# A two-layer graph kernel: bias products in half rows, and another order of the first group's set-up

## The chip, the core and the metric

The kernel runs on one core of a Trainium2 chip. Its time is the device time of one execution in microseconds (us); lower is better. The median of three runs of the kernel before is 1076.81 us (1076.48 to 1078.67).

A core has five engines with queues of their own: PE (TensorE, matrix products, with PEld for its weight loads), DVE (VectorE), ACT (ScalarE), POOL (GpSimd) and SP (SyncE, used here to issue DMAs only). Matrix products read SBUF and write PSUM.

## The reference

There are 128 graphs of 128 nodes with 64 features. Cut to what matters, for each graph:

```python
h   = relu(layernorm(x))
mask = adj > 0
z   = relu(h_j @ W1a + (h_j - h_k) @ W1b + b1)      # for every pair j, k; 192 wide
hm  = sum over k of mask[j, k] * z[j, k]
x   = x + hm @ W2 + deg[j] * b2
h   = relu(layernorm(x))
x   = x + (adj @ h) @ W.T
```

About one in eight of the adjacency entries is nonzero, so a row j has some 16 neighbours k.

## The kernel before

The 128 graphs are worked in 32 groups of G = 4. Inside a group, z is not computed for all pairs. Each quarter of 32 nodes k gives a row j up to D = 6 slots, and one-hot tiles S select the neighbour of each slot; neighbours beyond the sixth become "extra edges" (tiles R, RT, S2, X).

The group's main work is a list of T = 24 jobs. A job's `fill` lets TensorE form 768 columns of slot sums from the stacked tiles k3 and S3 (`g<-S,k` and `g<-id,k` in the profile); its `drain` reduces them on DVE (kind 0, `hm<-g`) or on ACT and then POOL (kind 1, `T<-g`, `T<-T`). Jobs of kind 1 use products 64 columns wide, two side by side. Three buffers of PSUM (`gtile`) are shared by the jobs, by the projections `pp` and by `pr`.

Between the jobs, pieces of other stages are run by three tables that name a job index and functions: AHEAD (set-up of the next group), OWN (extra edges of this group) and BEHIND (the finish of the group before). The set-up functions, in AHEAD's order, are:

- `pre_adj`: transposes the adjacency (`pt`), copies it (`adjT`), makes the mask (`maskT`), takes the statistics of x (`norm_a`)
- `pre_norm`: the normalised h
- `pre_rank`, `pre_slots`: the rank of each neighbour in its quarter (`pq`, `qs`), overflow `ov`, six slot tiles `S`, and 12 DMAs on SP's queue that copy S to `S3`
- `pre_hT`, `pre_count`: h transposed (`hT`); degree and number of overflows per row (`pd`, copied to `dn`, `nb`)
- `pre_proj` for r = 0 and 1: h times the joined weights `wp` (448 columns, float32), plus a bias product; split in three bfloat16 parts `ca` by ACT, DVE and POOL
- `pre_stack`: 12 DMAs on SP's queue that copy `ca` to `k3`, by quarter q and then by part
- `pre_edge_a`, `pre_place`, `pre_edge_b`, `pre_edge_d`, `pre_ra`, `pre_pads`, `pre_edge_c`: one-hot tiles of extra edges and corrections

TensorE's instructions are kept in the program's order (`mm`, `tp`, lines 181 and 184); the instructions of the other engines are put in order by the scheduler of the tile framework. Before the first job, all of AHEAD is run for group 0, one function after the other, after the weights have been loaded by 14 DMAs on ACT's queue and joined on DVE and TensorE.

The bias product adds `bias` to the projection exactly: its three bfloat16 parts stand in rows 0, 32 and 64 of `biasp`, the other rows are zero, and a tile of ones `oneb` sums over all 128 rows. It is run once for each half p of the partitions, after the two products with `wp`, which use 64 rows each:

```python
for p in range(2):
    s = slice(p * F, (p + 1) * F)
    mm(pp[:, p, 0 : 2 * H + O], d["hT"][s, r], wp[s, :], start=True, stop=False, ...)
for p in range(2):
    mm(pp[:, p, H : 2 * H + O], oneb, biasp, start=False, stop=True, ...)
```

Of the kernel before, what the change touches and what calls it, by code (L numbers as in the profile page):

```python
# [8 lines left out]
F32 = mybir.dt.float32  # L9
# [141 lines left out]
def kernel(  # L151
# [26 lines left out]
    nc = tc.nc  # L178
# [4 lines left out]
    def tp(*args, **kw):  # L183
        return tc.keep_in_program_order(nc.tensor.transpose(*args, **kw))  # L184
# [24 lines left out]
    with ExitStack() as main:  # L209
# [11 lines left out]
        def mtile(name):  # L221
            return ps_m.tile([P, 512], F32, tag="m", name=name)


        ident = const.tile([P, P], F32, tag="ident", name="ident")
        make_identity(nc, ident)
        identb = const.tile([P, P], BF16, tag="identb", name="identb")
# [8 lines left out]
        eps = const.tile([P, 1], F32, tag="eps", name="eps")  # L236
        nc.gpsimd.memset(eps, EPS)
# [27 lines left out]
        nc.vector.tensor_scalar(ioe, iov, BIG, None, ALU.add)  # L265


        wa2 = const.tile([P, H], F32, tag="wa2", name="wa2")
        wb2 = const.tile([P, H], F32, tag="wb2", name="wb2")
        w2a = const.tile([C0, O], F32, tag="w2a", name="w2a")  # L270
        w2h = const.tile([C0, O], F32, tag="w2h", name="w2h")
        w2bd = const.tile([P, 2, O], F32, tag="w2bd", name="w2bd")
        wl1 = const.tile([P, P], F32, tag="wl1", name="wl1")
# [5 lines left out]
        nc.vector.memset(w2bd, 0.0)  # L279
        nc.vector.memset(wl1, 0.0)  # L280
        for p in range(2):
            s = slice(p * F, (p + 1) * F)
            nc.scalar.dma_start(wa2[s, :], W1[0:F, :])
            nc.scalar.dma_start(wb2[s, :], W1[F : 2 * F, :])
            nc.scalar.dma_start(w2bd[s, p, :], W2[C0:H, :])
            nc.scalar.dma_start(wl1[s, s], W)
            nc.scalar.dma_start(b1d[s, :], b1[C0:H].unsqueeze(1))
        nc.scalar.dma_start(w2a, W2[0:C0, :])
        nc.scalar.dma_start(b2s, b2.unsqueeze(0).to_broadcast([P, O]))
        nc.scalar.dma_start(bias[:, 0:H], b1.unsqueeze(0).to_broadcast([P, H]))  # L290
        nc.scalar.dma_start(b1c, b1[0:C0].unsqueeze(1))
        nc.vector.tensor_scalar(w2h, w2a, 0.5, None, ALU.mult)

        wp = const.tile([P, 2 * H + O], F32, tag="wp", name="wp")
        wab = wp[:, H : 2 * H]
        nc.vector.tensor_scalar(wp[:, 0:H], wb2, -1.0, None, ALU.mult)
        nc.vector.tensor_tensor(wab, wa2, wb2, ALU.add)
        pw = mtile("pw")
        tp(pw[:, 0:P], wab[:, 0:C0], ident)
        wT = one.tile([P, P], F32, tag="wT", name="wT")  # L300
        nc.vector.tensor_copy(wT, pw[:, 0:P])
        pc = mtile("pc")
        mm(pc[:, 0:O], wT, w2h, start=True, stop=True)
        nc.vector.tensor_copy(wp[:, 2 * H : 2 * H + O], pc[:, 0:O])
        b1x = one.tile([P, P], F32, tag="b1x", name="b1x")
        nc.vector.tensor_copy(b1x, b1c.to_broadcast([P, P]))
        pb = mtile("pb")
        mm(pb[:, 0:O], b1x, w2h, start=True, stop=True)
        nc.vector.tensor_tensor(bias[:, H : H + O], pb[:, 0:O], b2s, ALU.add)
        pl = mtile("pl")  # L310
        tp(pl[:, 0:P], wl1, ident)
        nc.vector.tensor_copy(wl1t, pl[:, 0:P])

        biasp = const.tile([P, H + O], BF16, tag="biasp", name="biasp")
        nc.vector.memset(biasp, 0.0)
        left = bias
        for i in range(3):
            pt = one.tile([P, H + O], BF16, tag=f"bp{i}", name=f"bp{i}")
            nc.vector.tensor_copy(pt, left)
            nc.vector.tensor_copy(biasp[i * 32 : i * 32 + 1, :], pt[i * 32 : i * 32 + 1, :])  # L320
            if i < 2:
                nxt = one.tile([P, H + O], F32, tag=f"br{i}", name=f"br{i}")
                nc.vector.tensor_tensor(nxt, left, pt, ALU.subtract)
                left = nxt

        groups: dict[int, dict] = {}

# [15 lines left out]
        def norm_b(src, mv, to, u):  # L343

            sd = tmp.tile([P, G], F32, tag="sd", name=f"sd{u}")
            nc.scalar.activation(sd, mv[:, :, 1], AF.Sqrt, bias=eps)
# [17 lines left out]
        def pre_adj(g):  # L364
            d = groups[g]
            pt = mtile(f"pt{g}")
            for b in range(G):
                tp(pt[:, b * N : (b + 1) * N], d["adj"][:, b, :], ident)
            d["adjT"] = grp.tile([P, G, N], F32, tag="adjT", name=f"adjT{g}", bufs=3)
            nc.scalar.activation(  # L370
                d["adjT"].rearrange("k b j -> k (b j)"), pt, AF.Copy
            )
            d["maskT"] = grp.tile([P, G, N], BF16, tag="maskT", name=f"maskT{g}")
            nc.vector.tensor_scalar(d["maskT"], d["adjT"], 0.0, None, ALU.is_gt)
            d["mv"] = norm_a(d["x"], f"a{g}")

        def pre_norm(g):
            d = groups[g]
# [47 lines left out]
        def pre_count(g):  # L426
            d = groups[g]

            pd = mtile(f"pd{g}")
            for b in range(G):  # L430
                mm(
                    pd[:, b : b + 1], d["maskT"][:, b, :], oneb[:, 0:1], start=True, stop=True
                )
                mm(
                    pd[:, G + b : G + b + 1], d["ov"][:, b, :], oneb[:, 0:1], start=True, stop=True
                )
            d["dn"] = grp.tile([P, 2, G], F32, tag="dn", name=f"dn{g}")
            nc.vector.tensor_copy(d["dn"].rearrange("j t b -> j (t b)"), pd[:, 0 : 2 * G])  # L438
            d["nb"] = tmp.tile([P, G], BF16, tag="nb", name=f"nb{g}")
            nc.vector.tensor_copy(d["nb"], d["dn"][:, 1])  # L440

        def pre_pads(g):
            d = groups[g]
# [16 lines left out]
        def pre_proj(g, r):  # L460
# [7 lines left out]
            for p in range(2):  # L468
# [3 lines left out]
                    start=True, stop=False, skip_group_check=True,  # L472
                )
            for p in range(2):
                mm(
                    pp[:, p, H : 2 * H + O], oneb, biasp,
                    start=False, stop=True, skip_group_check=True,
                )
            x = pp[:, :, 0 : 2 * H].rearrange("n p (t u) -> n p t u", t=2)
# [16 lines left out]
        def pre_stack(g):  # L496

            d = groups[g]
            d["k3"] = grp.tile([K3, Q, 2, G, H], BF16, tag="k3", name=f"k3{g}")
            for q in range(Q):  # L500
                for part in range(3):
                    nc.sync.dma_start(
                        d["k3"][part * QN : (part + 1) * QN, q],
                        d["ca"][q * QN : (q + 1) * QN, part],
                    )
# [28 lines left out]
        def pre_edge_a(g):  # L534
            d = groups[g]
            pv = mtile(f"pv{g}")
            mm(pv[:, 0:G], upb, d["nb"], start=True, stop=True)
            mm(pv[:, G : 2 * G], oneb, d["nb"], start=True, stop=True)
            nc.vector.tensor_tensor(ovf, ovf, pv[:, G : 2 * G], ALU.max)

            d["half"] = tmp.tile([P, G], F32, tag="half", name=f"half{g}")
            nc.vector.tensor_scalar(d["half"], d["dn"][:, 1], -0.5, 0.5, ALU.mult, ALU.add)
# [276 lines left out]
        def pieces(table, t, g):  # L819
            if 0 <= g < NG:  # L820
                for f in table.get(t, ()):
                    f(g)
# [54 lines left out]
```

## Time and profile before

| | before |
|---|---|
| median of three runs, us | 1076.81 |
| the profiled execution's own time, us | 1076.04 |
| its span (first to last instruction), us | 1074.3 |
| mean granted TensorE clock | 0.987 |
| PE busy, us (share) | 1035.5 (96%) |
| PEld busy | 731.8 (68%) |
| DVE busy | 843.3 (79%) |
| ACT busy | 684.1 (64%) |
| POOL busy | 717.6 (67%) |
| PE instructions | 10438 products, 10438 weight loads |

Some groups of the page: `g<-S,k` 2048 products, 383.4 us; `g<-id,k` 4096, 381.3; `pp<-wp,hT` 256, 67.8; `pp<-biasp,oneb` 128, 25.3 (mean 280 ns). A float32 product appears as two passes. The durations of products overlap, as each is counted from its issue to its modelled end; the starts tell the pace. Some DMA rows, from issue to landing: S 192 KB, 4.0 us; k 96 KB, 2.2; adj 256 KB, 2.8; x 128 KB, 2.7; bias 96 KB, 4.1; b1c 0.5 KB, 3.9; b2s 32 KB, 3.6; wa 48 KB, 2.8; wb 48 KB, 3.1.

In a view's rows, L181 and L184 are the two helpers that record every product and transpose, so a product is told by its tiles. "SPq" is SP's queue issuing a DMA, "[0.29 <-PE pb L181]" an idle time before an instruction and what ended it.

### The profile page before, as it was taken

The numbers are of one execution on the slowest core, as the hardware profiler recorded it, in microseconds if no ns is written. First come the engines' busy times: TensorE is split into PE (matmuls) and PEld (weight loads), VectorE is DVE, ScalarE is ACT, GpSimd is POOL, SyncE is SP. The second block draws the span as 40 slices with busy tenths as digits, with TensorE's granted clock in tenths as the row PEclk, the third lists the DMA queues.
The fourth block names the chain that finished last, engine by engine and source line by source line (L and its number), as shares of the span: only waits on it lengthen the run. The fifth ranks groups of instructions, "written<-read, shape, count | busy, mean of one in ns | idle before, by whom it ended". The sixth has DMA issues, their size and how long they took to land.

```text
span 1074.3 us, 27146 instructions
## 1 busy us (share of the span) xinstructions
PE 1035.5 (96%) x10438; PEld 731.8 (68%) x10438; DVE 843.3 (79%) x1955; ACT 684.1 (64%) x1473; POOL 717.6 (67%) x810
## 2 busy tenths in 40 slices
PE   3699999999999999999999999999999999999995
PEld 1477776777677677677677677677777777667773
DVE  5468888878888878887877888877888887888763
ACT  4366666676666677666667666667666667666652
POOL 1377666777666687666686766677766677666674
PEclk9799999999999999999999999999999999999998
DMA  4456655456655456655456655445665545664420
GB/s 104 114 138 144 140 126 115 112 130 149 138 125 124 111 120 153 141 124 134 102 118 147 143 131 130 114 112 138 144 142 125 115 114 127 146 141 109 108 66 13
DMA packets 89062, 132.29 MB, mean 123 GB/s; under 512 B 47584, under 2 KB 64352, under 8 KB 88928
## 3 DMA queue, kind: packets, MB, share of 16 engines
q1 hardware_dynamic: 87552, 130.08, 53.0%
q8 instruction: 84, 1.38, 0.5%
q10 hardware_dynamic: 1376, 0.43, 0.2%
q14 instruction: 50, 0.41, 0.1%
HBM read 13.01 MB, written 4.19 MB: 16 GB/s over the span
## 4 chain that ended last, share of the span: by engine, by line
PE 93%; DVE 2%; SPq 2%; DMA 1%; ACT 1%; POOL 1%; issue 0%; ACTq 0%; POOLq 0%; DVEq 0%
PE g L181 49%; PE pe L181 7%; PE pp L181 7%; PE py L181 7%; PE px L181 6%; PE pr L181 3%; PE po L181 2%; PE pga L181 2%; PE pn L181 2%; PE pt L184 1%; PE pj L181 1%; PE pgq L181 1%; PE pq L181 1%; SPq L407 1%; DVE S L401 1%; PE pty L184 1%
## 5 line engine op out<-in xcount | busy, mean ns | idle before, releaser
L761 DVE TENSOR_REDUCE hm<-g 128x64 f32<-128x768 f32 x512 | 469.8, 949 | 115.7 <-PE g L181 113.5
L784 POOL TENSOR_TENSOR T<-T 128x768 f32<-128x768 f32 (+2 forms) x384 | 442.1, 1151 | 144.4 <-ACT T L771 126.8
L181 PEld LDWEIGHTS <-k 96*128 96x128 bf16 (+1 forms) x6144 | 408.5, 103 | 150.7 <-issue 37.2
L181 PE MATMUL g<-S,k 96*128 96x384 bf16 (+1 forms) x2048 | 383.4, 331 | 6.3 <-DMA k<-ca 5.1
L181 PE MATMUL g<-id,k 96*128 96x192 bf16 (+1 forms) x4096 | 381.3, 246 | 0.0
L771 ACT ACTIVATE T<-g 128x768 f32<-128x768 f32 x256 | 202.9, 805 | 25.4 <-PE g L181 23.4
L494 POOL TENSOR_TENSOR ca<-rest,ca 128x768 bf16<-128x768 f32 x64 | 105.0, 1642 | 170.5 <-ACT ca L493 161.1
L401 DVE TENSOR_SCALAR S<-qs 128x512 bf16<-128x512 bf16 x192 | 116.5, 675 | 3.0 <-issue 0.5
L483 ACT ACTIVATE ca<-pp 128x768 bf16<-128x768 f32 x64 | 51.3, 801 | 102.9 <-PE pp L181 99.0
L181 PE MATMUL pe<-RT,X 128*128 128x128 f32 (+1 forms) x512 | 79.4, 299 | 0.0
L493 ACT ACTIVATE ca<-rest 128x768 bf16<-128x768 f32 x64 | 53.7, 840 | 25.1 <-DVE rest L485 25.1
L181 PE MATMUL pp<-wp,hT 64*128 64x448 f32 x256 | 67.8, 607 | 1.9 <-DVE dn L438 1.9
L485 DVE TENSOR_TENSOR rest<-pp,ca 128x768 f32<-128x768 f32 x64 | 59.9, 936 | 4.5 <-ACT ca L483 4.5
L181 PEld LDWEIGHTS pe<-RT,X 128*128 128x128 f32 (+1 forms) x512 | 52.1, 164 | 9.8 <-issue 5.2
L668 ACT ACTIVATE ys<-py 128x256 f32<-128x256 f32 x32 | 12.3, 383 | 65.8 <-PE py L181 65.8
L456 POOL TENSOR_TENSOR ra<-ra,np 64x256 f32<-64x256 f32 x64 | 51.6, 806 | 2.4
L181 PE MATMUL px<-ca,S 128*128 128x192 bf16 x384 | 53.0, 247 | 0.0
L181 PE MATMUL px<-ca,R 128*128 128x192 bf16 x384 | 52.6, 246 | 0.0
L181 PEld LDWEIGHTS <-oneb 128*128 128x128 bf16 x192 | 13.5, 97 | 56.1 <-issue 56.1
L352 ACT ACTIVATE h<-x,mra,rsa 128x64 f32<-128x64 f32 x128 | 48.8, 435 | 3.7 <-DVE mra L350 2.2
L612 ACT ACTIVATE X<-px 128x256 f32<-128x256 f32 x64 | 24.5, 383 | 38.7 <-PE px L181 34.9
L181 PEld LDWEIGHTS <-R 128*128 128x128 bf16 x512 | 43.6, 98 | 7.9 <-issue 0.6
(130 smaller groups left out, 1425.0 us busy)
## 6 DMA issues: line engine op xcount, KB each, us to landing
S<-S SPq DMA_DIRECT2D x384, 192.0 KB, 4.0
k<-ca SPq DMA_DIRECT2D x384, 96.0 KB, 2.2
adj<-in_adj_dram SPq DMA_DIRECT2D x32, 256.0 KB, 2.8
x<-in_x_dram SPq DMA_DIRECT2D x32, 128.0 KB, 2.7
out_dram<-ot SPq DMA_DIRECT2D x32, 128.0 KB, 2.0
wa<-in_L_gnn_W_dram ACTq DMA_DIRECT2D x2, 48.0 KB, 2.8
wb<-in_L_gnn_W_dram ACTq DMA_DIRECT2D x2, 48.0 KB, 3.1
bias<-in_L_gnn_b_dram ACTq DMA_DIRECT2D x1, 96.0 KB, 4.1
```

Of the source, the lines that this page charges most:

```text
L181: return tc.keep_in_program_order(nc.tensor.matmul(*args, **kw))
L352: nc.scalar.activation(to(b), src[:, b, :], AF.Relu, bias=mr[:, b : b + 1], scale=rs[:, b : b + 1])
L401: nc.vector.tensor_scalar(d["S"][:, i, :], d["qs"].rearrange("k b j -> k (b j)"), float(i) + BIG, None, ALU.is_equal,)
L456: nc.gpsimd.tensor_tensor(d["ra1"][s], d["ra1"][s], d["np0"][s, 2 * p : 2 * p + 2], ALU.mult)
L483: nc.scalar.activation(parts[0], x, AF.Copy)
L485: nc.vector.tensor_tensor(rest, x, parts[0], ALU.subtract)
L493: nc.scalar.activation(parts[1], rest, AF.Copy)
L494: nc.gpsimd.tensor_tensor(parts[2], rest, parts[1], ALU.subtract)
L612: nc.scalar.activation(d["X"][:, r::2, 0:C0], pxv[:, :, 0:C0], AF.Abs)
L761: nc.vector.tensor_reduce(d["hm0"][:, qp, b, js], self.gt[:, :, 0:ND].rearrange("h i (d j) -> h j i d", d=D), AX.XY, ALU.add, apply_absolu ...
L771: nc.scalar.activation(d[key][:, qp].rearrange("h (i d) j -> h i d j", i=2), self.gt[:, :, 0:ND].rearrange("h i (d j) -> h i d j", d=D), A ...
L784: nc.gpsimd.tensor_tensor(t[:, 0:n], t[:, 0:n], t[:, n : 2 * n], ALU.add)
```

## The change

- The bias product is run on 64 rows for each half p: `oneb[s]` and `biasp[s]`. The three parts of the bias now stand in rows 0, 1, 2 and again 64, 65, 66, placed by a product with the column i of `id64` (ones in rows i and 64 + i).
- The weights are loaded by 12 DMAs on SP's queue, after x and adj of group 0, in another order; W1 comes as one tile `w1` with both halves side by side. The joining of weights is split in `weights_a`, `weights_b`, `weights_c`, which stand between the set-up functions of group 0.
- The set-up of group 0 is written out by hand. Of group 1, `pre_adj`, `pre_norm` and `pre_hT` are run before the first job; of group 0, `pre_edge_b`, `pre_edge_c`, `pre_edge_d`, `pre_ra` and `pre_pads` are run after jobs 0, 1, 2, 4 and 5. x and adj of group 1 are loaded at that earlier place.
- A square root on one column stands at the top, and the memsets of `w2bd` and `wl1` and of `eps` are moved up.
- `pre_stack` copies by part, then by quarter.
- `nb` and `half` are computed from `pd` in PSUM instead of from `dn`; `half` moves from `pre_edge_a` to `pre_count`.

```diff
+        eps = const.tile([P, 1], F32, tag="eps", name="eps")
+        nc.gpsimd.memset(eps, EPS)
+        first = const.tile([P, 1], F32, tag="first", name="first")
+        nc.scalar.activation(first, eps, AF.Sqrt)
...
+        id64 = const.tile([P, 4], F32, tag="id64", name="id64")
+        nc.vector.tensor_tensor(id64, ident[:, 0:4], ident[:, F : F + 4], ALU.add)
...
-        for p in range(2):
-            s = slice(p * F, (p + 1) * F)
-            nc.scalar.dma_start(wa2[s, :], W1[0:F, :])
-            nc.scalar.dma_start(wb2[s, :], W1[F : 2 * F, :])
...
+        def weight_loads():
+            nc.sync.dma_start(w2a, W2[0:C0, :])
+            nc.sync.dma_start(b1c, b1[0:C0].unsqueeze(1))
+            for p in range(2):
+                s = slice(p * F, (p + 1) * F)
+                nc.sync.dma_start(w1[s], W1.rearrange("(t f) h -> f t h", t=2))
+            nc.sync.dma_start(bias[:, 0:H], b1.unsqueeze(0).to_broadcast([P, H]))
+            nc.sync.dma_start(b2s, b2.unsqueeze(0).to_broadcast([P, O]))
+            for p in range(2):
+                s = slice(p * F, (p + 1) * F)
+                nc.sync.dma_start(w2bd[s, p, :], W2[C0:H, :])
+                nc.sync.dma_start(wl1[s, s], W)
+                nc.sync.dma_start(b1d[s, :], b1[C0:H].unsqueeze(1))
...
+        def weights_b():
...
+                if i == 0:
+                    nc.vector.tensor_scalar(biasp, pt, id64[:, i : i + 1], None, ALU.mult)
+                else:
+                    nc.vector.scalar_tensor_tensor(
+                        biasp, pt, id64[:, i : i + 1], biasp, ALU.mult, ALU.add
+                    )
...
-            nc.vector.tensor_copy(d["nb"], d["dn"][:, 1])
+            nc.vector.tensor_copy(d["nb"], pd[:, G : 2 * G])
+            d["half"] = tmp.tile([P, G], F32, tag="half", name=f"half{g}")
+            nc.vector.tensor_scalar(
+                d["half"], pd[:, G : 2 * G], -0.5, 0.5, ALU.mult, ALU.add
+            )
...
             for p in range(2):
-                mm(
-                    pp[:, p, H : 2 * H + O], oneb, biasp,
+                s = slice(p * F, (p + 1) * F)
+                mm(
+                    pp[:, p, H : 2 * H + O], oneb[s, :], biasp[s, :],
                     start=False, stop=True, skip_group_check=True,
                 )
...
-            for q in range(Q):
-                for part in range(3):
+            for part in range(3):
+                for q in range(Q):
...
         load(0)
-        for t in range(T):
-            pieces(AHEAD, t, 0)
+        weight_loads()
+        pre_adj(0)
+        weights_a()
+        pre_norm(0)
+        pre_rank(0)
+        pre_slots(0)
+        weights_b()
+        pre_hT(0)
+        pre_count(0)
+        load(1)
+        pre_proj(0, 0)
+        pre_proj(0, 1)
+        pre_stack(0)
+        early = {(f, 1) for f in (pre_adj, pre_norm, pre_hT)}
+        pre_adj(1)
+        pre_edge_a(0)
+        pre_place(0)
+        pre_norm(1)
+        pre_hT(1)
+        weights_c()
+        FIRST = {0: pre_edge_b, 1: pre_edge_c, 2: pre_edge_d, 4: pre_ra, 5: pre_pads}
         for g in range(NG):
-            if g + 1 < NG:
+            if 0 < g < NG - 1:
                 load(g + 1)
...
                 job.drain()
+                if g == 0 and t in FIRST:
+                    FIRST[t](0)
                 pieces(OWN, t, g)
```

`weights_a` holds the joins behind `wp` (products `pw`, `pc`), `weights_b` those behind `bias` and `biasp` (product `pb`), `weights_c` the transpose of W (`pl`).

More of the change, by code (lines that the diff above doesn't have):

```diff
@@ L222, in mtile @@
             return ps_m.tile([P, 512], F32, tag="m", name=name)
+        eps = const.tile([P, 1], F32, tag="eps", name="eps")
+        nc.gpsimd.memset(eps, EPS)
+        first = const.tile([P, 1], F32, tag="first", name="first")
+        nc.scalar.activation(first, eps, AF.Sqrt)
+        w2bd = const.tile([P, 2, O], F32, tag="w2bd", name="w2bd")
+        nc.vector.memset(w2bd, 0.0)
+        wl1 = const.tile([P, P], F32, tag="wl1", name="wl1")
+        nc.vector.memset(wl1, 0.0)
         ident = const.tile([P, P], F32, tag="ident", name="ident")
@@ L235 @@
         nc.vector.tensor_copy(id3, id32)
-        eps = const.tile([P, 1], F32, tag="eps", name="eps")
-        nc.gpsimd.memset(eps, EPS)
+        id64 = const.tile([P, 4], F32, tag="id64", name="id64")
+        nc.vector.tensor_tensor(id64, ident[:, 0:4], ident[:, F : F + 4], ALU.add)
         ones = const.tile([P, P], F32, tag="ones", name="ones")
@@ L265 @@
         nc.vector.tensor_scalar(ioe, iov, BIG, None, ALU.add)
-        wa2 = const.tile([P, H], F32, tag="wa2", name="wa2")
-        wb2 = const.tile([P, H], F32, tag="wb2", name="wb2")
+        w1 = const.tile([P, 2, H], F32, tag="w1", name="w1")
         w2a = const.tile([C0, O], F32, tag="w2a", name="w2a")
         w2h = const.tile([C0, O], F32, tag="w2h", name="w2h")
-        w2bd = const.tile([P, 2, O], F32, tag="w2bd", name="w2bd")
-        wl1 = const.tile([P, P], F32, tag="wl1", name="wl1")
         wl1t = const.tile([P, P], F32, tag="wl1t", name="wl1t")
@@ L278 @@
         bias = const.tile([P, H + O], F32, tag="bias", name="bias")
-        nc.vector.memset(w2bd, 0.0)
-        nc.vector.memset(wl1, 0.0)
-        for p in range(2):
-            s = slice(p * F, (p + 1) * F)
-            nc.scalar.dma_start(wa2[s, :], W1[0:F, :])
-            nc.scalar.dma_start(wb2[s, :], W1[F : 2 * F, :])
-            nc.scalar.dma_start(w2bd[s, p, :], W2[C0:H, :])
-            nc.scalar.dma_start(wl1[s, s], W)
-            nc.scalar.dma_start(b1d[s, :], b1[C0:H].unsqueeze(1))
@@ L288 @@
[L288 to L292, printed above, removed]
         wp = const.tile([P, 2 * H + O], F32, tag="wp", name="wp")
         wab = wp[:, H : 2 * H]
-        nc.vector.tensor_scalar(wp[:, 0:H], wb2, -1.0, None, ALU.mult)
-        nc.vector.tensor_tensor(wab, wa2, wb2, ALU.add)
@@ L298 @@
[L298 to L312, printed above, removed]
-        biasp = const.tile([P, H + O], BF16, tag="biasp", name="biasp")
[L315 to L324, printed above, removed]
+        biasp = const.tile([P, H + O], BF16, tag="biasp", name="biasp")
@@ new lines, in weights_a @@
+        def weights_a():
+            nc.vector.tensor_tensor(wab, w1[:, 0], w1[:, 1], ALU.add)
+            nc.vector.tensor_scalar(wp[:, 0:H], w1[:, 1], -1.0, None, ALU.mult)
+            nc.vector.tensor_scalar(w2h, w2a, 0.5, None, ALU.mult)
+            pw = mtile("pw")
+            tp(pw[:, 0:P], wab[:, 0:C0], ident)
+            wT = one.tile([P, P], F32, tag="wT", name="wT")
+            nc.vector.tensor_copy(wT, pw[:, 0:P])
+            pc = mtile("pc")
+            mm(pc[:, 0:O], wT, w2h, start=True, stop=True)
+            nc.vector.tensor_copy(wp[:, 2 * H : 2 * H + O], pc[:, 0:O])
@@ new lines, in weights_b @@
+        def weights_b():
+            b1x = one.tile([P, P], F32, tag="b1x", name="b1x")
+            nc.vector.tensor_copy(b1x, b1c.to_broadcast([P, P]))
+            pb = mtile("pb")
+            mm(pb[:, 0:O], b1x, w2h, start=True, stop=True)
+            nc.vector.tensor_tensor(bias[:, H : H + O], pb[:, 0:O], b2s, ALU.add)
+            left = bias
+            for i in range(3):
+                pt = one.tile([P, H + O], BF16, tag=f"bp{i}", name=f"bp{i}")
+                nc.vector.tensor_copy(pt, left)
+                if i == 0:
[4 more added lines that the diff above has]
+                    )
+                if i < 2:
+                    nxt = one.tile([P, H + O], F32, tag=f"br{i}", name=f"br{i}")
+                    nc.vector.tensor_tensor(nxt, left, pt, ALU.subtract)
+                    left = nxt
@@ L326, with weights_c @@
+        def weights_c():
+            pl = mtile("pl")
+            tp(pl[:, 0:P], wl1, ident)
+            nc.vector.tensor_copy(wl1t, pl[:, 0:P])
         groups: dict[int, dict] = {}
@@ L345, in norm_b @@
             sd = tmp.tile([P, G], F32, tag="sd", name=f"sd{u}")
-            nc.scalar.activation(sd, mv[:, :, 1], AF.Sqrt, bias=eps)
+            sq = nc.scalar.activation(sd, mv[:, :, 1], AF.Sqrt, bias=eps)
+            if u == "a1":
+                tc.keep_in_program_order(sq)
             rs = tmp.tile([P, G], F32, tag="rs", name=f"rs{u}")
@@ L374, in pre_adj @@
             nc.vector.tensor_scalar(d["maskT"], d["adjT"], 0.0, None, ALU.is_gt)
-            d["mv"] = norm_a(d["x"], f"a{g}")
+            if "mv" not in d:
+                d["mv"] = norm_a(d["x"], f"a{g}")
         def pre_norm(g):
@@ L539, in pre_edge_a @@
             nc.vector.tensor_tensor(ovf, ovf, pv[:, G : 2 * G], ALU.max)
-            d["half"] = tmp.tile([P, G], F32, tag="half", name=f"half{g}")
-            nc.vector.tensor_scalar(d["half"], d["dn"][:, 1], -0.5, 0.5, ALU.mult, ALU.add)
             mid = tmp.tile([P, G], F32, tag="mid", name=f"mid{g}")
@@ L821, in pieces @@
                 for f in table.get(t, ()):
-                    f(g)
+                    if (f, g) not in early:
+                        f(g)
         load(0)
-        for t in range(T):
-            pieces(AHEAD, t, 0)
+        weight_loads()
[19 more added lines that the diff above has]
+        FIRST = {0: pre_edge_b, 1: pre_edge_c, 2: pre_edge_d, 4: pre_ra, 5: pre_pads}
         for g in range(NG):
-            if g + 1 < NG:
+            if 0 < g < NG - 1:
                 load(g + 1)
```

## The prediction

> **What bounds the kernel now.** I read the page's slices first, then the table of windows for one middle group, then TensorE's waits, then the chain of waits for the start, and last TensorE's timeline around one projection.
>
> ```profile
> PE   3699999999999999999999999999999999999995
> ```
> ```profile
> 500.00:532.00 32.00, 31.98 (x328) 22.69 (x326) 26.29 (x61) 21.37 (x46) 22.39 (x25) 1.00 0.54 123
> ```
> ```profile
> PE g L181 <- DVE e L489: 0.5, 1, 0.5
> ```
>
> The window row (us, then busy time of PE, PEld, DVE, ACT, POOL, granted clock, DMA share, GB/s) shows a group: 31.98 of 32.00 us on TensorE at full clock, the next engine (VectorE) at 26.29. The wait row is the only one TensorE has between 75 and 1040 us: 0.5 us. From group 1 on, what TensorE is spared is therefore the end's gain, and 5.7 us per group lie between it and the next engine. The slices (40 of 26.9 us, in tenths) show the other piece: TensorE at 3, then 6 tenths in the first two. The chain of waits tells why (start, us, what):
>
> ```profile
> 9.41 3.91 DMA b1c<-in_L_gnn_b_dram
> ...
> 16.97 0.60 PE pq L181
> 17.59 0.60 ACT qs L391
> 18.22 0.29 DVE ov L394
> 18.51 1.21 DVE S L401 x6
> ...
> 37.69 2.22 DMA k<-ca
> ```
> ```profile
> 19.75 10.21 SPq L407 DMA_DIRECT2D S<-S  x12
> 30.06 8.22 SPq L502 DMA_DIRECT2D k<-ca  x12
> ```
>
> Weights issued one by one on ACT's queue, b1c the last at 9.41, hold the program-ordered TensorE (pw, pc, pb, pl ahead of the first adjacency transpose) until 14.6 us. Then the slots S are ready at 19.73, and 24 copies on SP's queue take 19.75 to 38.28, the last landing at 39.91. So first full speed is **S plus 20.2 us**.
>
> **Part 1, bias products in half rows** (L475 of before). TensorE's timeline at group 2:
>
> ```profile
> 84.56 1.02 PE L181 MATMUL pp<-wp,hT 64*128 64x448 f32 x4
> 85.52 0.39 PE L181 MATMUL pp<-biasp,oneb 128*128 128x256 bf16 x2
> 85.75 0.49 PE L181 MATMUL g<-S,k 96*128 96x384 bf16 x2
> 86.07 0.49 PE L181 MATMUL g<-id,k 96*128 96x192 bf16 x4
> ...
> 87.08 1.02 PE L181 MATMUL pp<-wp,hT 64*128 64x448 f32 x4
> 88.04 0.39 PE L181 MATMUL pp<-biasp,oneb 128*128 128x256 bf16 x2
> 88.36 0.52 PE L181 MATMUL g<-S,k 96*64 96x384 bf16 x4
> ```
> ```profile
> 85.04 0.54 PE L181 MATMUL pp<-wp,hT 64*128 64x448 f32 x2
> ```
>
> Read starts, not durations. Two g<-S of 384 columns take 86.07-85.75 = 0.32, so a bf16 column streams in 0.417 ns and a 256-column bias product in 0.107; two one after another are the 0.23 from 85.52 to 85.75. Before the 64-column job of kind 1 the same pair takes 0.32: 0.09 more is what a change of the array's division costs. The f32 products are half-row already: their two passes start together, two by two (x2 at 84.56, x2 at 85.04). A f32 transpose of 128 columns takes 0.11 (four in 0.44 in the chain), so two cycles a column and 448 columns 0.37; the 0.48 from 85.04 to 85.52 holds a change of division too, 0.10. With half-row bias products there is none between pp and bias, and the two halves run side by side as the f32 ones do: pp's end, 0.11 + 0.01, then one change 0.10. First projection of a group: 0.10+0.23 = 0.33 becomes 0.22, saving 0.11. Second: 0.10+0.32 = 0.42 becomes 0.21, saving 0.21. Per group **0.32**, for the 31 groups whose projections lie under TensorE's full load: **-10.0 us**.
>
> The rule that speaks against: the Trainium skill's "TensorE: Matmul & The Clock Gate", Part 3, "The mechanism", says that a weight load overlaps a running matmul only when it goes to other rows of the array. Both halves of oneb go to rows on which a f32 pass is streaming; by the rule about 0.10 (an oneb load is 97 ns in the page's groups) is exposed in each projection, leaving 0.12 per group, -3.8 us in all. The trace is against it here: all four f32 loads of 84.56 lie within 84.56 to 84.86 (PEld's row: 0.30 for x4), the second pair of passes starts at 85.04 behind streams on those same rows with no load between. I take the row; -3.8 stays in the range.
>
> **Part 2, the start.** Removed from the path to S: pl, the three row copies, and the place of all weights' products before the transposes. Order of the changed program: SP issues x0, adj0, 12 weight DMAs (one fewer pair, since W1 comes as two), x1, adj1, x2, adj2, then the 24 copies. At 0.55 us each, as ACT's issues took, and with waits on earlier landings (the program reuses a DMA's semaphore eight DMAs later, so each waits for the one eight before it), x1 goes out near 8.4, after the bias row's landing (4.0 + 4.1 from the page's table), and adj2 near 10: SP is free before S. ACT: the table load (1.28) and a first Sqrt run at the top, norm of x0 to 6.9 (four of 0.43), adjT 7.5. adj0 landed at 5.35 before (the third x load waited for it), so its transposes end near 6.4. DVE, in order: b1x behind b1c (issued 2.4 + 3.9 = 6.3), wab and wp behind w1 (3.5 + 3.1 = 6.6) to 7.4; identb to triq, 1.7 before plus id64, to 9.2; wT 9.4, maskT 9.75. PE: pc, then pq 9.8 to 10.4; ACT qs to 11.0. **Then a new wait**: DVE's next is a batch statistic of x1, landing 8.4 + about 3.2 = 11.6 (x loads took 2.5 and 4.0 at the start). Behind it stand bias, bp, ov, S: 0.2+0.2+0.2+0.25+0.3+1.25 = 2.3. S is ready at 13.9 (13.2 to 14.9 for x1's two landings), against 19.73: **-5.9 us**, if the 24 copies then run as before. They should: the first half moves 12 x 192 KB in 10.2 us (DMA share 1.01 in the window 25 to 30), later k copies at 0.59. Their data are ready: the biasp steps, now three DVE operations on 128x256 at 0.26 to 0.42 (nearest rows bp and br), follow S to 16.5; pp to 19.1, parts 0 by 20, parts 1 by 22.2, POOL's parts 2 by 24.1, while SP reaches k only at 24.1.
>
> **Part 3, copies by part.** At the start the last copy is as late as before, so job 1 is unchanged; job 0 starts later (needs copies 9 and 10) without moving job 1's end. In a middle group the last k copy is issued 1.2 us or more before the next group's first job takes its last quarter, and no wait for k stands in PE's list after 75 us. Nothing gained or lost; if the copies came late it is rival D.
>
> **Part 4, what moves into group 0.** From the idle start into its jobs: prt 0.22, pgq 0.33, pr 1.21, pn 0.54; out of them: pt 0.44, ph 0.22. Net +1.64 of TensorE. But group 0 waits for DVE already:
>
> ```profile
> 52.38 1.02 PE L181 MATMUL pp<-wp,hT 64*128 64x448 f32 x4 [1.89 <-DVE dn L438]
> ```
> ```profile
> 38.00:43.00 5.00, 3.42 (x16) 2.45 (x17) 1.48 (x2) 0.00 (x0) 0.00 (x0) 0.50 0.31 72
> 52.00:57.00 5.00, 4.62 (x24) 2.42 (x24) 4.31 (x11) 1.09 (x2) 0.59 (x2) 0.68 0.87 178
> ```
>
> pp waited for the reductions behind six S operations that took 3.72 instead of 1.30 beside POOL's additions; and the granted clock was 0.50 and 0.68 there. Some added matmuls fill the 1.89; against that ra's 1.64 and X stand ahead of qs on ACT, so S of group 1 comes about 1.2 later relative to the jobs. Between +0.3 and +2.5 I take **+1.0**, near the wait as it stands; both low-clock stretches I assume again.
>
> **Part 5, counts from PSUM.** nb and half read pd: 0.16 to 0.17 each like dn from PSUM (0.16), on an engine with 5.7 us spare. Zero; no row shows a loss beyond 0.05 per group, also hidden.
>
> **Sum.** Profiled run 1076.04 = span 1074.3 + 1.74 around it. -10.0 -5.9 +1.0 = -14.9: **1061.1** against the profiled run; its median is 0.8 higher, within the spread, so I say 1061.2. The tail behind TensorE (POOL additions, last norm) is not touched.
>
> **Rivals.**
> A (0.66): as above, 1058 to 1064.
> B (0.15): half rows give little, because loads are exposed as by the rule or the halves do not run together. Against: the f32 pairs. Exposed loads: -3.8 for -10.0, 1067.3; one after another with only one change saved, 0.09 x 31 = -2.8: 1068.3.
> C (0.14): the start gains only half, S at 17, since SP's weights or x1 land late (b1c and x1 both took 3.9 once): 1064.2.
> D (0.05): **slower**. Copies by part leave the last piece of every quarter to the last four copies. Copy 12 was issued at 420.94 in group 12 and lands 2.3 later at 423.2; its job starts at 424.55: 1.3 slack, 1.0 after part 1's shrinkage. Only if it lands 1.5 later in each group does 0.5 x 31 = 15.5 eat everything: 1076.7, and worse beyond. For it: POOL's part 2 ends at 414.0 with S copies issued to 412.4. Against: in the new order that part is first wanted near 418.
>
> B and C together still give 1071. A measurement of this kernel tells 0.2% (2 us) from no change. Range 1057 to 1068 takes in A's bounds, C and most of B. Faster is A, B and C but for 0.01, of which with D's near side come 0.02 for same, and 0.04 remain for slower: 0.94, 0.02, 0.04.
>
> **What would show it.** Right: bias products 64 rows high, two starting within 0.02; 0.21 less in g to g over a second projection, period 31.66; the first S copy near 13.9; no k wait past group 0. Wrong: a gap of 0.1 between pp and bias, the first S copy after 16, DVE standing at x1's statistic for over 2 us, or PE waits for k in later groups.

## The result, and the profile after

| | before | after |
|---|---|---|
| median, us | 1076.91 (1076.12 to 1078.67, 6 runs) | 1073.49 (1072.33 to 1074.08, 6 runs) |
| ratio to before, 95% interval | | 0.9964 [0.9951, 0.9977] |
| profiled execution, us | 1076.04 | 1073.18 |
| its span, us | 1074.3 | 1071.6 |
| first `pt` to next `pt` of a middle group, us | 31.96 | 31.83 |

The change is faster by 3.4 us, and the interval leaves 1 out; 15 were forecast. (Three of e12's six executions below, the profiled one among them, took over 1.5% longer than its fastest; its ratio is that of the other three.) The page's slices and its shares of the chain that ended last, after:

```profile
PE   4699999999999999999999999999999999999995
...
PE 79%; DVE 15%; issue 2%; ACT 1%; SPq 1%; POOL 1%; DMA 1%; POOLq 0%; DVEq 0%; ACTq 0%
```

The row for one middle group in the table of windows (us; then busy time of PE, PEld, DVE, ACT, POOL; granted clock; DMA share; GB/s):

```profile
500.00:532.00 32.00, 31.80 (x329) 22.71 (x330) 26.28 (x61) 21.53 (x47) 22.43 (x25) 1.00 0.55 126
```

TensorE still looks full and VectorE's mean still shows 5.7 us of room, yet VectorE holds 15% of the chain. The two timelines that say why follow. First TensorE after, around both projections of group 2 (start, us, engine, line, operation, tiles, count):

```profile
83.78 1.02 PE L181 MATMUL pp<-wp,hT 64*128 64x448 f32 x4
84.64 0.28 PE L181 MATMUL pp<-biasp,oneb 64*128 64x256 bf16 x2
84.84 0.50 PE L181 MATMUL g<-S,k 96*128 96x384 bf16 x2
...
86.19 1.02 PE L181 MATMUL pp<-wp,hT 64*128 64x448 f32 x4
87.05 0.28 PE L181 MATMUL pp<-biasp,oneb 64*128 64x256 bf16 x2
87.45 0.52 PE L181 MATMUL g<-S,k 96*64 96x384 bf16 x4
```

The half rows do what was said: 64 rows high, the pair as one (0.28 for both). No weight load is exposed: both loads of `oneb` start at 84.26, while `pp` still runs, 0.38 ahead of their products. From `pp` to the next `g` the first projection takes 84.84 - 83.78 = 1.06 (1.19 before). The second takes 87.45 - 86.19 = 1.26 against 1.28: here 0.21 was due, and 0.02 came. What stands there is a wait; the rows are those of the weight loads' waits, 75 to 1040 us (sum, times, longest), before and after:

```profile
PEld L181 <- DVE e L489: 6.8, 29, 0.8
PEld L181 <- DVE e L517: 21.2, 30, 1.3
```

These sums overstate it, as loads run ahead of the products, but they name `e`: job 10 takes the PSUM buffer of the first projection, which `e` frees last. VectorE's timeline of before, then of after, in that stretch:

```profile
82.93 0.96 DVE L761 TENSOR_REDUCE hm<-g 128x64 f32<-128x768 f32 x1
...
86.52 0.36 DVE L340 BATCH_NORM_AGGREGATE mvb<-stb 128x2 f32<-128x6 f32 x4
86.80 0.13 DVE L542 TENSOR_SCALAR half<-dn 128x4 f32<-128x4 f32 x1
86.85 0.22 DVE L338 BATCH_NORM_STATS2 sta<-x 128x6 f32<-128x64 f32 x1
86.98 0.94 DVE L485 TENSOR_TENSOR rest<-pp,ca 128x768 f32<-128x768 f32 x1
87.84 0.46 DVE L489 SCALAR_TENSOR_TENSOR e<-pp,dn,x 128x64 f32<-128x64 f32 x2
88.22 0.94 DVE L761 TENSOR_REDUCE hm<-g 128x64 f32<-128x768 f32 x1
```
```profile
82.15 0.96 DVE L787 TENSOR_REDUCE hm<-g 128x64 f32<-128x768 f32 x1
...
85.81 0.36 DVE L359 BATCH_NORM_AGGREGATE mvb<-stb 128x2 f32<-128x6 f32 x4
86.09 0.93 DVE L513 TENSOR_TENSOR rest<-pp,ca 128x768 f32<-128x768 f32 x1
86.93 0.47 DVE L517 SCALAR_TENSOR_TENSOR e<-pp,dn,x 128x64 f32<-128x64 f32 x2
87.31 0.95 DVE L787 TENSOR_REDUCE hm<-g 128x64 f32<-128x768 f32 x1
```

In both, with the rows left out here, each operation starts before the one ahead of it has ended: from job 6's reduction to job 9's, VectorE works in order and never rests, 88.22 - 82.93 = 5.29 us before, 87.31 - 82.15 = 5.16 after. Job 11 takes the buffer that the last of these reductions frees (it ends at 88.26 after, and job 11 starts at 88.31), so this chain sets how soon TensorE goes on. It is 0.13 shorter after: before, a statistic of a later group (`sta` at 86.85) stands ahead of `rest`; after, it does not. 0.13 is the whole gain of a group.

The start is as forecast. SP's timeline, after:

```profile
13.88 10.23 SPq L429 DMA_DIRECT2D S<-S  x12
24.21 8.19 SPq L530 DMA_DIRECT2D k<-ca  x12
```

The copies of S begin at 13.88, against 19.75. But group 0 gives it back. Timeline after, 44 to 51 us (idle time and its releaser in brackets):

```profile
44.71 5.33 DVE L423 TENSOR_SCALAR S<-qs 128x512 bf16<-128x512 bf16 x6
...
46.86 1.31 POOL L480 TENSOR_TENSOR ra<-ra,np 128x512 f32<-128x512 f32 x1
...
50.97 1.87 PE L181 MATMUL pp<-wp,hT 64*128 64x448 f32 x4 [3.29 <-DVE hm L787]
```

The six S operations take 5.33 (3.72 before) beside POOL's additions, now with those of `ra` among them, and they start 3.0 later after job 1's `g<-id,k` (10.35 against 7.33). `pp` waits 3.29 (1.89). From job 1's `g<-id,k` (40.32 before, 34.36 after) to the bias product of the second projection that group 0 runs (57.43, 56.77) it is 17.11 before and 22.41 after.

**The ledger**, in us of the two spans: start 34.36 - 40.32 = -5.96; group 0 22.41 - 17.11 = +5.30; from that bias product to the last one of its kind (57.43 to 1015.51, 56.77 to 1011.12) -3.73; the end behind it 60.48 - 58.79 = +1.69. Sum -2.70, which is 1071.6 - 1074.3.

### The profile page after: what moved, and what is told of

It reads as the page before. It is cut to its first block, busy times and chain, and to the rows that moved or that the text cites. A ratio compares the mean times of both kernels' runs of the same rounds, so it can differ in the third digit from the quotient of the medians.

```text
span 1071.6 us, 27079 instructions
## 1 busy us (share of the span) xinstructions
PE 1026.6 (96%) x10406; PEld 729.7 (68%) x10438; DVE 847.8 (79%) x1955; ACT 684.7 (64%) x1474; POOL 718.7 (67%) x810
## 4 chain that ended last, share of the span: by engine, by line
PE 79%; DVE 15%; issue 2%; ACT 1%; SPq 1%; POOL 1%; DMA 1%; POOLq 0%; DVEq 0%; ACTq 0%
PE g L181 45%; DVE hm L787 8%; PE py L181 7%; PE px L181 6%; PE pe L181 6%; PE pr L181 4%; PE po L181 2%; PE pga L181 2%; DVE stb L357 1%; DVE e L517 1%; PE pt L184 1%; PE pj L181 1%; PE prt L181 1%; DVE S L423 1%; PE pgq L181 1%
## 5 line engine op out<-in xcount | busy, mean ns | idle before, releaser
L423 DVE TENSOR_SCALAR S<-qs 128x512 bf16<-128x512 bf16 x192 | 119.0, 688 | 2.9 <-issue 0.5
L812 POOL TENSOR_TENSOR hm<-T 128x64 f32<-128x64 f32 x128 | 41.1, 321 | 10.0
```

Of the source, the lines that this page charges most:

```text
L423: nc.vector.tensor_scalar(d["S"][:, i, :], d["qs"].rearrange("k b j -> k (b j)"), float(i) + BIG, None, ALU.is_equal,)
L812: nc.gpsimd.tensor_tensor(d["hm1"][:, b, js], t[:, 0], t[:, 2], ALU.add)
```

## The experiments

A period is the distance of first `pt` in middle groups. Ratios are to the kernel before, run on the same chip.

### Which part gives the 0.13 per group

`e1_half_rows_alone`: the kernel before with the half-row bias products and the `biasp` they need, nothing else.

```diff
-                    pp[:, p, H : 2 * H + O], oneb, biasp,
+                    pp[:, p, H : 2 * H + O], oneb[s, :], biasp[s, :],
```

> The kernel before with the half-row bias products alone; its start and the order of VectorE's work are those of before. Theory (VectorE's chain from the end of job 6 to the release of the first projection's PSUM is as long as TensorE's work beside it, 5.43 us, so TensorE's saving there is waited away): the group's period falls from 31.96 by no more than 0.06, the time is 1075 to 1077. Rival 1 (the bias products give what the changed kernel's period shows, 0.125 per group): 1073.1. Rival 2 (the forecast's 0.32 per group): 1067.

1076.23, ratio 0.9995 [0.9987, 1.0004], period 31.96: nothing. Its row of TensorE's waits, 75 to 1040 us; the same row of before, shown with the prediction, read 0.5 us, once:

```profile
PE g L181 <- DVE e L496: 8.3, 30, 0.8
```

`e2_full_rows_in_after`: the changed kernel with all 128 rows.

> The changed kernel with the bias products back on all 128 rows; VectorE's order as in the changed kernel, with one batch statistic less ahead of the first projection's drain. Theory: TensorE sets the period again, 31.96, so 30 x 0.125 = 3.8 us over the changed kernel, about 1077.2, no better than before though its start is 5.9 us earlier. Rival (the new start is worth several us by itself and the bias products little): 1071 to 1074.

1073.87, 0.9975 [0.9966, 0.9984], period 31.85. My expectation missed: the half rows bring 0.02 per group, and the gain comes from elsewhere in the change. In the profile of before, job 11 already stood a little behind VectorE:

```profile
88.71 0.50 PE L181 MATMUL g<-id,k 96*64 96x192 bf16 x8
89.22 0.52 PE L181 MATMUL g<-S,k 96*64 96x384 bf16 x4
```

From job 10's last products to job 11's first it is 0.51; in e8 below, where job 11 does not wait, it is 0.33. Job 9's reduction ends at 89.16.

`e5_counts_alone`: before, with `nb` and `half` read from PSUM. `e6_counts_undone`: after, with both read from `dn` again and `half` back in `pre_edge_a`.

```diff
-            nc.vector.tensor_copy(d["nb"], d["dn"][:, 1])
+            nc.vector.tensor_copy(d["nb"], pd[:, G : 2 * G])
+            nc.vector.tensor_scalar(d["half"], pd[:, G : 2 * G], -0.5, 0.5, ALU.mult, ALU.add)
```

> The kernel before with the counts read from PSUM alone (nb and half from pd, half in pre_count). Theory (VectorE's chain from job 6 to job 11 sets the period of both kernels, and what shortens it is that the scheduler now puts one batch statistic of 0.13 us behind the drains): period 31.85 instead of 31.96, 30 x 0.11 = 3.3 us less, 1073.5. Rival (the counts cost and bring nothing, as forecast; the 0.13 per group come from the bias products): period 31.96, 1076.8.

> The changed kernel with nb and half computed from dn again, half in pre_edge_a; half rows, start and copies as changed. Theory: the statistic comes back into VectorE's chain, the period is 31.96 again in spite of the half rows, 3.8 us over the changed kernel, 1077.3. Rival: 1073 to 1074, period 31.84.

e5: 1073.2, 0.997 [0.996, 0.9979], period 31.85. e6: 1077.28, 1.0001 [0.9993, 1.001], period 31.96. Both as expected. Of the 0.13 of every group the counts alone bring 0.11, and with them alone the kernel before is as fast as with the whole change. It is not their price: read from PSUM or from `dn` they take 0.13 to 0.16. It is the order that comes with them: in e5 `sta` stands behind `rest` and `e` (at 89.05, `rest` at 86.52), in e6 ahead of them again (84.91, 85.05). Why the scheduler places it so stays open.

### Taking VectorE's chain apart: new waits

`e3_post1_later` moves `post1` (the addition to x and its statistics) out of the stretch, from job 7 to job 12.

```diff
-            7: (post1,),
+            12: (post1,),
```

> The changed kernel with post1 (an addition and eight statistics, 1.2 us of VectorE) moved from after job 7 to after job 12, out of VectorE's chain. Theory: the chain falls to about 4.1 us, TensorE sets the period, and the whole saving of the half rows shows: 31.96 - 0.32 = 31.64, 0.19 x 30 = 5.7 less than the changed kernel, 1067.8; the gap of about 0.37 before the 64-column job after the second projection falls to 0.10. Rival (what waits there is not VectorE's chain, or the 1.2 us block another drain later): 1072 to 1075, gap unchanged or moved.

1109.99, 1.031 [1.0296, 1.0324], period 33.05: 42 us above the forecast. The chain of waits in a middle group:

```profile
515.56 1.06 PE pp L181 x6
516.62 1.49 PE g L181 x24
...
524.00 1.17 ACT et L573 x4
525.17 1.39 ACT T L797 x2
526.56 1.00 ACT h L373 x3
...
527.60 0.77 PE pga L181 x6
```

One part came as forecast: with `post1` out of the way, the second projection takes 1.06 from `pp` to `g`, where it took 1.28 before. But TensorE now has two other waits (sums from 75 to 1040 us): 16.0 us in 29 waits for `hm`, as the moved block stands ahead of later reductions, and 6.0 us in 29 for `h` in `pga`, as the statistics come late and meet ACT's other work.

`e7_stats_later_half_rows` moves the statistics alone, to job 10, with `post3` at 21 and VectorE's `rest` and these statistics in program order; `e8_stats_later_full_rows` is the same in full rows. `e9_stats_between_drains` puts them at job 9 in the kernel e4 below, `e10_post2_early` adds `post2` at job 9, and `e11_post2_early_full_rows` is e10 in full rows.

```diff
             7: (post1,),
-            18: (post2,),
-            19: (post3,),
+            10: (post1b,),
+            18: (post2,),
+            21: (post3,),
```

> The changed kernel with the eight statistics of post1 behind both projections' drains (kept there in program order), and post3 after job 21 instead of 19, since h2 is ready later. Theory: 0.8 us leave VectorE's chain, TensorE sets the period, the half rows show whole: 31.96 less 0.085 (the wait before job 11, in the gap of 182 against 97 ns) less 0.32 = 31.55; 30 x 0.28 = 8.5 below the changed kernel, 1065. Rival (another wait takes over at once, as when post1 went to job 12): period 31.8 or more.

> The same with bias products on all 128 rows. Theory: TensorE sets the period at 31.96 - 0.085 = 31.87, so 0.32 over its partner, some 9.6 us in all, 1074.5. Rival (the half rows save nothing at all): equal to its partner.

> Both repairs: the first group's edge pieces before job 0, and the eight statistics of post1 between the drains of the first and the second projection (post2 and post3 in their places). Theory (VectorE's chain to job 11 is 0.8 us shorter; ScalarE's h still stands ahead of the edge tiles, so the wait of pgq for R stays about as in the run with the statistics behind both drains, 0.3): period 31.8, 1067 to 1068, no better than the edge pieces alone. Rival (the chain to job 11 is all there is): period 31.55, 1059.5.

> The same with post2 at once after the statistics (job 9 instead of 18), so that ScalarE forms h before the edge tiles. Theory: neither the chain to job 11 nor R waits, TensorE sets the period at 31.55 to 31.65, 30 x 0.2 to 0.28 below the run with the edge pieces alone, 1060 to 1062. Rival (VectorE stands at the reciprocal of ScalarE's root ahead of the second drain, and job 12 waits): 31.8 or more, 1067 or more.

> The same as the run with post2 early, with bias products on all 128 rows. Theory: if TensorE sets the period in both, 0.32 per group more than its partner, 9.6 us. If another wait sets the partner's period, less: 0 to 7 us.

| | time, us | ratio | period | TensorE waits for |
|---|---|---|---|---|
| e7 | 1074.19 | 0.9971 [0.996, 0.9983] | 31.82 | R |
| e8 | 1079.36 | 1.0027 [1.0019, 1.0035] | 32.05 | R |
| e9 | 1087.99 | 1.0097 [1.0082, 1.0111] | 32.50 | h |
| e10 | 1077.98 | 1.0008 [1.0, 1.0017] | 32.16 | hm |
| e11 | 1080.93 | 1.0038 [1.0023, 1.0053] | 32.27 | hm |

e7, e9 and e10 missed by 9 us and more, e8 by 5; e11 is 3 us over e10, within the 0 to 7 that were allowed for another wait. Rows of TensorE's waits, 75 to 1040 us, of e7, e9 and e10:

```profile
PE pgq L181 <- ACT R L603: 7.1, 30, 0.2
```
```profile
PE pga L181 <- ACT h L375: 8.2, 30, 0.4
```
```profile
PE g L181 <- DVE hm L794: 4.6, 30, 0.2
```

In e7 and e9 ACT is late, with `h` ahead of `R` or late itself; in e10 VectorE stands 0.22 at `rsb`, which waits for ACT's `sdb`, with the second `rest` and four reductions behind it. So in none of these kernels were the 5.7 us of mean slack to be had by moving statistics. The pairs show something else: with the chain loosened, half rows are worth 32.05 - 31.82 = 0.23 and 32.27 - 32.16 = 0.11 per group.

### Group 0

`e4_edges_before_jobs`: the changed kernel, with the pieces of group 0's extra edges ahead of job 0.

```diff
-        FIRST = {0: pre_edge_b, 1: pre_edge_c, 2: pre_edge_d, 4: pre_ra, 5: pre_pads}
+        pre_edge_b(0)
+        pre_edge_d(0)
+        pre_ra(0)
+        pre_pads(0)
+        pre_edge_c(0)
+        FIRST = {}
```

> The changed kernel with the first group's edge pieces (edge b, c, d, ra, pads) run before job 0 as before, in TensorE's idle time of 26 to 32 us, and not between its jobs. Theory (they cost 5 us there: 2.3 us of TensorE, ra ahead of the next ranks on ScalarE, POOL's pad products beside VectorE's slots): the first full group is 3 to 4.5 us shorter, slots of group 1 take under 4 us instead of 5.33, time 1069 to 1070.5. Rival (the loss in group 0 is the low clock and comes anyway): 1072.5 to 1073.5.

1067.86, 0.9922 [0.9908, 0.9935], period 31.83; 1.1 below the range that I gave. Timeline of e4:

```profile
41.15 3.72 DVE L423 TENSOR_SCALAR S<-qs 128x512 bf16<-128x512 bf16 x6
...
45.80 1.02 PE L181 MATMUL pp<-wp,hT 64*128 64x448 f32 x4 [2.03 <-DVE hm L787]
```

S takes 3.72 again, `pp` waits 2.03 instead of 3.29 and runs at full pace (1.02 instead of 1.87). The place of these pieces cost 5.6 us: nearly all that the start had gained.

### Two operations less in VectorE's chain

`e12_counts_behind_chain`: e4 with `nb` and `half` made in `pre_edge_a`, behind both projections, and VectorE's order otherwise held as in e4 (with the statistics of x of the group after next behind `e`).

```diff
+            keep(nc.vector.tensor_copy(d["nb"], d["dn"][:, 1]))
+            keep(nc.vector.tensor_scalar(d["half"], d["dn"][:, 1], -0.5, 0.5, ALU.mult, ALU.add))
```

> e4_edges_before_jobs with nb and half computed from dn behind the second projection (in pre_edge_a) instead of ahead of job 7's reduction, and with VectorE's order otherwise held as it is there (reductions, rest, e, the statistics of x1 and rsb kept in the program's order; the statistics of the group after next computed behind e). Between job 6's reduction and job 9's, VectorE then has two operations of 0.07 us less, and nothing in their place. If VectorE's chain from job 6 to job 11 sets the period, as I hold, the period falls from 31.83 by 0.14 to 31.69 (TensorE's own work in such a group is 31.55), and the time by 29 x 0.14 = 4.1, to 1063.8. Rival 1: another wait already lies close behind and takes it, as in e7, e9 and e10: period 31.8 or more, 1067 or more. Rival 2: that the two operations are too small to matter and only whole statistics or reductions shift the period: 1067.9.

Ratio 1.1447 [1.1413, 1.148]: a large miss. Its timeline:

```profile
509.08 0.98 DVE L579 CAST nb<-dn 128x4 bf16<-128x4 f32 x1
...
510.11 0.17 PE L183 MATMUL pv<-nb,upb 128*128 128x4 bf16 x1 [2.54 <-DVE nb L579]
```

I had overlooked that `pv`, next in TensorE's order, reads `nb`, which now stood behind two more reductions, and `nb` took 0.98 instead of 0.15. On top of the 2.5 us in each group the granted clock fell in many of them (below).

`e13_counts_behind_rsb` puts both right behind `rsb`, ahead of the second `rest`.

> e12_counts_behind_chain with nb and half computed from dn right behind rsb, so ahead of the second rest and the second e (in e12 they stood behind two more reductions, and TensorE's pv, next in its order, waited 2.5 us for nb in each group), and with mrb behind the second e, where it stands in e4. In e12 the distance from job 6's reduction to job 10 had shrunk as meant, and 34.40 us, its period at full clock, less the 2.71 that pv's gap had grown, is 31.69. Theory (VectorE's chain from job 6 to job 11 sets the period): 31.69, and 1067.86 - 29 x 0.14 = 1063.8. Rival 1: a further wait lies just behind it: 31.8 or more, 1067 or more. Rival 2: pv still waits for nb: 32 or more, above 1073.

1103.8, 1.0259 [1.0245, 1.0273], period 33.06: a miss again. VectorE's timeline, and POOL's:

```profile
511.94 1.04 DVE L586 CAST nb<-dn 128x4 bf16<-128x4 f32 x1
...
514.22 1.04 DVE L379 SCALAR_TENSOR_TENSOR mrb<-mvb,rsb 128x4 f32<-128x4 f32 x1
```
```profile
511.31 1.64 POOL L543 TENSOR_TENSOR ca<-rest,ca 128x768 bf16<-128x768 f32 x1 [4.24 <-DMA S<-S]
513.43 1.81 POOL L849 TENSOR_TENSOR T<-T 128x768 f32<-128x768 f32 x1 [0.47 <-ACT T L836]
```

`nb` ends at 512.98, POOL's `ca` at 512.95; `mrb` at 515.26, POOL's `T` at 515.24. An operation of 0.15 waits until POOL's running one is done.

`e14_counts_on_act` takes both off VectorE: ScalarE makes them from PSUM, while it waits for the projection. `e15_counts_on_act_full_rows` is the same with bias products over 128 rows.

```diff
+            nc.scalar.activation(d["nb"], pd[:, G : 2 * G], AF.Copy)
+            nc.scalar.activation(d["half"], pd[:, G : 2 * G], AF.Copy, bias=0.5, scale=-0.5)
```

> As e13_counts_behind_rsb, but nb and half are made by ScalarE from pd in PSUM, right behind hT, where ScalarE waits for the projection anyway; VectorE's order is that of e4 without these two. In e12 and e13 nb, read from SBUF, took 1.0 us instead of 0.15: it ended when GpSimd's running operation ended (e13: nb 511.94 to 512.98, GpSimd's ca 511.31 to 512.95), and so did mrb; here neither stands beside a running GpSimd operation in the way they did there. Theory (VectorE's chain from job 6 to job 11 sets the period): 31.69, 1067.86 - 29 x 0.14 = 1063.8. Rival 1: a further wait lies just behind: 31.8 or more, 1067 or more. Rival 2: ScalarE, delayed by two operations of about 0.2, makes the first ca late and with it rest and e: 31.9, 1070.

> e14_counts_on_act with the bias products over all 128 rows again. With VectorE's chain 0.14 shorter, TensorE has less slack left to lose in: the half rows are then worth what of their 0.32 per group is not waited away. Theory: TensorE's own time is 31.55 in half rows and about 31.85 in full rows, so the period is about 31.85, 0.16 over its partner, and the time 0.16 x 29 = 4.6 more: 1068.4. If half rows were worth nothing even then (the rival to the prediction's Part 1), the two are equal within 0.03 in the period.

e14: 1062.28, 0.9868 [0.9853, 0.9883], period 31.69. e15: 1068.14, 0.992 [0.9906, 0.9933], period 31.85. Both periods are as the theory had them; e14's time lies 1.5 below its forecast. TensorE's timeline of e14 at the second projection:

```profile
490.42 1.02 PE L183 MATMUL pp<-wp,hT 64*128 64x448 f32 x4
491.27 0.28 PE L183 MATMUL pp<-biasp,oneb 64*128 64x256 bf16 x2
491.54 0.52 PE L183 MATMUL g<-S,k 96*64 96x384 bf16 x4
```

From `pp` to `g` it is now 1.12 (after 1.26, before 1.28). Two operations of 0.07 each, taken from an engine busy 79% of the time, moved each group by their full 0.14. (e14 also keeps e12's and e13's held order, which was not run by itself; but from job 6's reduction to job 9's its list is e4's less the two counts, 491.40 - 486.38 = 5.02 against 5.17.) With the chain that much shorter the half rows are worth 31.85 - 31.69 = 0.16. e14 is the fastest kernel of the case.

## Why the prediction was wrong

The direction was right, the size was not: 1073.5 against 1061.2 (1057 to 1068).

- **What bounds the kernel: the step that failed.** "What TensorE is spared is therefore the end's gain, and 5.7 us per group lie between it and the next engine" took a mean over 32 us for room in every part of it. From job 6 to job 11 VectorE had none: in e14 the period follows VectorE's chain one to one (0.14 for 0.14), in e1 TensorE's saving went into a wait (8.3 us in 30 waits). TensorE's wait row of before (0.5 us) did not show it: TensorE's own work there came out nearly level with the chain, and the 0.18 at job 11 is not in that row. The weight loads' row, 6.8 us in 29 waits for `e`, was a hint. The view I left out was VectorE's timeline beside TensorE's, in the stretch where the saving lay.
- **Part 1.** As TensorE's own work the -10.0 (31 x 0.32 is 9.9) was near: 1.19 to 1.06 at the first projection against a forecast 0.11, and at the second 1.28 to 1.06 in e3, where VectorE is not late there, against 0.21. As the end's gain it was nil by itself (e1), 0.02 per group in the changed kernel (e2), and at most 0.23 in any pair (e7 and e8). Rival B's -3.8 is close to what the later groups gained, but by luck: its mechanism, exposed loads, did not occur, and the gain came from Part 5. The row was rightly preferred to the rule there.
- **Part 2** was right: first copy at 13.88 against 13.9, -5.96 against -5.9. The new wait, VectorE at the statistic of x1, was there as named, 1.93 long. That the number fits to 0.1 is luck in part: x1 went out at 9.24 and not 8.4, but landed 2.50 later and not 3.2; and the six terms behind it add up to 2.4, not 2.3, and took 2.1. Rival C is out.
- **Part 3** was right: no wait for k in later groups, D did not come.
- **Part 4** was mis-sized: +1.0 (0.3 to 2.5), measured +5.3. I counted TensorE's added products and ACT's order, and took S at 3.72 and the slow stretches as they stood. By the trace, S starts 3.0 later after job 1 (1.2 forecast: `ra` stands ahead of `qs` on ACT, and the added products come while TensorE runs at half pace), takes 1.6 longer, with `ra`'s additions on POOL beside it, and behind the longer wait the stretch of the two projections is 0.75 longer (granted clock from 52 to 57 us 0.55, before 0.68). Together that is the 5.3; e4 gives it back.
- **Part 5**, costed at zero, was nearly the whole gain in later groups: 0.11 of the 0.13 per group (e5), by what it did to VectorE's order. I had the two orders of instructions to compare and looked for what the counts cost, not for what changed places around them.
- **The tail** was to be untouched. The span ends 5.7 us after the last `ot` instead of 4.3, and no row accounts for that 1.5. It stays open: in e1 and e5, with the start of before, and in e3 it is 4.4 to 4.5, in the others 5.5 to 6.3.

After the misses of e12 and e13, the point forecasts for e14 and e15 (1063.8 and 1068.4; measured 1062.28 and 1068.14) came from adding up one engine's in-order list between two buffer releases. That is the sum that was missing.

## What to carry to other kernels

Before you count a saving on the busiest engine, follow who frees its next buffers, and add up that engine's list in order over that stretch alone; a mean share of 79% can hide a stretch at 100%. When a change touches small operations, compare the whole order of each engine, as a neighbour that changed places can be worth more than the operation. And a piece moved from an idle start into busy jobs costs what it collides with, not its own length.

## What was unexpected of the hardware

**Small VectorE operations wait for GpSimd.** In e12 and e13 `nb` (0.15 alone) took 0.98 and 1.04, the medians of 32, and in the groups shown it ended with POOL's operation, as did `mrb` in e13; the reductions from PSUM kept their 0.95 beside it, and `nb` read from PSUM took 0.15 in every group of after. The Trainium skill's "SBUF — State Buffer", "Who interferes with whom", has a rule for this: the two engines share one pair of SBUF ports. VectorE's copies, casts and `tensor_scalar` can take it for a whole instruction, one with two SBUF inputs contends with a GpSimd instruction that reads SBUF, and one with at most one SBUF input, outside the modes that use both pairs, does not. The trace agrees: the ends in e13 lie within 0.03 us of each other. S in group 0 (1.30 alone, 3.72 and 5.33 beside POOL) fits it, though no run here proved that S waits for the same reason.

**After waits of 2.5 us the clock fell to half.** e12's windows (us, PE busy, granted clock, DMA share, GB/s):

```profile
540.00:544.00 4.00, 1.96 (x21) 1.00 1.00 206
544.00:548.00 4.00, 3.49 (x33) 0.75 0.64 173
548.00:552.00 4.00, 4.00 (x28) 0.50 0.56 129
```

The wait there is the 2.55 of `pv` at 544.51. The clock stayed at 0.50 until past 560, while after the like wait at 508 it stayed at 1.00. e12's mean granted clock was 0.897 to 0.923 in all six executions, against 0.982 or more in every other kernel. The Trainium skill's "TensorE: Matmul & The Clock Gate", "HAM oscillation — how this bites in real kernels", puts the limit at idle gaps of more than about 3.4 us; here it fell behind waits of at most 2.55, in some groups and not in others.

**The clock column can miss it.** The window of 34 to 38 us of after (columns as above), and TensorE's timeline there:

```profile
34.00:38.00 4.00, 4.00 (x24) 3.09 (x24) 2.93 (x4) 0.60 (x1) 0.00 (x0) 1.00 0.32 87
```
```profile
33.72 0.85 PE L181 MATMUL g<-S,k 96*128 96x384 bf16 x2
34.36 0.85 PE L181 MATMUL g<-id,k 96*128 96x192 bf16 x4
35.00 0.63 PE L181 MATMUL prt<-identb,R 128*128 128x128 bf16 x4
```

The clock reads 1.00, yet each of the two groups of `g` products takes 0.64 to the next start, where full pace is 0.32. Why is open.
